# Axial attention: score matmuls for two groups at once, reciprocals spread by full-array matmuls, value loads issued by SyncE

## The chip, the cores and the metric

One Trainium2 chip, one core of it. The time is the device time of one execution in microseconds (us), as the median of several runs. The kernel is one launch; it computes four residual layers on a batch of four images with 256 channels of 64 x 64 pixels, all in float32 outside.

## The reference

Each layer is `x = x + f(groupnorm(x))`. The change concerns layer 0, an axial attention along the image's rows; the other three are 3x3 convolutions (one with ternary weights, one with binary activations, one with weights built from 4 x 4 scales). Cut to what matters:

```
q, k, v = bn1(einsum('nci,oc->noi', x, w_qkv))      # n = 256 rows of pixels, 16 groups,
                                                    # q and k 8 channels, v 16, i = 64 positions
qe = einsum('ngci,cij->ngij', q, q_emb)             # q_emb[c,i,j] = rel[c, i-j+63]
ke = einsum('ngci,cij->ngij', k, k_emb)
qk = einsum('ngki,ngkj->ngij', qe, ke)
sim = bn2(concat([qk, qe, ke], axis=1)).sum over the three
sim = softmax(sim, axis=3)                          # over j
attn   = einsum('ngij,ngcj->ngci', sim, v)
attn_e = einsum('ngij,cij->ngci', sim, v_emb)
out = bn3(concat([attn, attn_e])), the two halves added
```

The batch normalisations use the statistics of this batch, so each needs all of its input before it can be applied.

## The kernel before, in words

The program is written with a tile framework: the code issues instructions in a program order, a planner orders them per engine with that order as priority, and it puts in the semaphore waits. DMAs are issued from two queues, SP (SyncE, `nc.sync`) and ACT (ScalarE, `nc.scalar`); a DMA issued from ACT stands in line with ACT's own instructions. All DMAs of both queues share eight completion semaphores in turn, and each waits for the DMA before it on its own semaphore.

Scratch tensors in device memory (DRAM) carry data between the stages. A *pair* gp (0 to 7) is two of the sixteen groups, r = 0 and 1.

**Stage A** (L154 to L328, 0 to 317 us): group norm and the projection of q, k, v (L257). The projections of one image lie in `qs`, 128 partitions x 8 x 512, and are stored to `q_d` by sixteen DMAs from ACT (L295 to L299), one for each of two halves t (q and k channels) and eight l (the position i modulo 8). The values go to `vt_d`.

**Stage B** (L350 to L618, 317 to 1076 us): the products `qk`. `projections(j)` (L388) loads `qb` from `q_d` by two SP DMAs for four groups (L393), 32 DMAs in all, and DVE scales it (L399). `position_terms` multiplies with the relative embeddings `rm` into `pd` (PE, L434) and DVE transposes that into `t` (L441). `product` (L445 on) multiplies the transposed terms (PE, L453) into `pq`; ACT copies `pq` to the output tile `o` with a sum (L457) and squares it in place for a second sum (L462). `o` holds one pair of one image (128 partitions x 4096 numbers, 2 MB) and has two buffers (pool `op`), `pq` has two PSUM banks. There are 4 x 8 = 32 such tiles. A finished tile is stored to `qk_d` in four parts of 512 KB from ACT, one after each of the first four products of the next tile (`finish`, L522 to L527), and the last tile by one DMA of 2 MB (L559). The order of the loop (L535 to L556): position terms of half a tile, then two products of the half before, and so on. `term_sums` and the pieces of work called `jobs` (weights of a later layer) lie between.

**Stage C** (L621 to L893, 1076 to 1700 us): eight units, each one image and half of the pairs (four of them). A partition of the large tile `pt` is one group r of a pair and one position j, as 64 r + j; its columns are the pairs, rows n and positions i. In each unit:
- `scores(u, k)`, k = 0 to 7: `terms` (L676) loads `qc` by one SP DMA of 512 KB for two k and ACT applies the batch norm to it in eight activations (L687); SP loads `si`, 1 MB of `qk_d` (L699; three buffers, pool `cip`); PE adds the two embedding terms by sixteen matmuls of 32 rows x 64 columns of the array, 256 wide, for r = 0 and 1, two parities of i and four row groups of the array (L711, tile `e`); DVE adds `si` into `pt` (L723).
- `exponentials`: ACT, four activations for a k (L753). `sums`: PE adds up over the 64 j by matmuls with ones (L764, `den`).
- `reciprocals` (L771): DVE inverts `den`; PE spreads the result to the 16 channels of each group by 64 matmuls of 32 x 32 for each half h of a tile, in two PSUM tiles `pr` (L784); ACT copies it to `rb` (L789).
- `values` (PE L796) with the value matrices `vb`, `values_out` (DVE L805, then an ACT DMA to `at_d`), and `embedded` (PE L820, DVE L826) with the matrices `ve`.
- `load_values` (L663) loads the `vb` of the next unit by sixteen ACT DMAs of 128 KB (L667); they are called in fours between the `values_out` of this unit. `vb` is zeroed once by POOL (L637).

The order: scores of the next unit are interleaved with `embedded` of this one. `cnt` (L653) holds two constant matrices, `ones` for the sums and `pick` for the spreading. A second version of stage C with shifted exponentials (`general`) stands behind a branch that isn't taken here. The convolutions follow from 1700 us to the end.

Of the kernel before, what the change touches and what calls it, by code (L numbers as in the profile page):

```python
# [32 lines left out]
M_ID, M_GRP, M_GRPS, M_ALL, M_TKC, M_KTC, M_SHUF, M_ODD, M_N = 0, 1, 2, 3, 4, 6, 8, 9, 10  # L33

GROUPS = [0, 1, 2, 3, 8, 9, 10, 11, 4, 5, 6, 7, 12, 13, 14, 15]


@with_exitstack
def network(ctx: ExitStack, tc, x, wqkv, relm, relt, relw, relv, counts, masks, vecs, rowv, ab, w1, l2w1, l2w2, l3w, mats, out):
# [12 lines left out]
    q_d = [scratch(f"q_d{b}", [8, 2, 8, G, 512]) for b in range(B)]  # L52
# [84 lines left out]
    def kernel_rows(u, w, a, c):  # L137

        v = nc.vector
        v.tensor_scalar(u[:, 0], w[:, 0], 0.25, None, ALU.mult)  # L140
        v.tensor_copy(u[:, 5], w[:, 2])
        v.tensor_tensor(a, w[:, 0], w[:, 2], ALU.add)
        v.tensor_tensor(u[:, 1], a, w[:, 1], ALU.add)
        v.tensor_tensor(u[:, 2], a, w[:, 1], ALU.subtract)
        v.tensor_scalar(u[:, 1:3], u[:, 1:3], -1.0 / 6, None, ALU.mult)
        v.scalar_tensor_tensor(c, w[:, 2], 4.0, w[:, 0], ALU.mult, ALU.add)
        v.scalar_tensor_tensor(u[:, 3], w[:, 1], 2.0, c, ALU.mult, ALU.add)
        v.scalar_tensor_tensor(u[:, 4], w[:, 1], -2.0, c, ALU.mult, ALU.add)
        v.tensor_scalar(u[:, 3:5], u[:, 3:5], 1.0 / 24, None, ALU.mult)

# [5 lines left out]
    with ExitStack() as ph:  # L156
# [86 lines left out]
        for b in range(B):  # L243
# [51 lines left out]
            for t in range(2):  # L295
                for l in range(8):
                    nc.scalar.dma_start(
                        out=q_d[b][l, t].rearrange("c g f -> g c f"), in_=qs[t][:, l].rearrange("p a h -> p (a h)")
                    )  # L299
# [30 lines left out]
    def spread_scales(sp, psp, xs, order, tag="pst"):  # L330


        ps = psp.tile([P, 2, G], F32, name=fresh(tag), tag=tag)
        for t in range(2):
            r = small(sp, [P, 2, G])
            for i in range(2):
                nc.vector.tensor_scalar(r[:, i, :], msk, xs[t][:, i : i + 1], None, ALU.mult)
            nc.tensor.matmul(
                ps.rearrange("p i g -> p (i g)"), lhsT=mt[:, order + t, :], rhs=r.rearrange("p i g -> p (i g)"),
                start=(t == 0), stop=(t == 1),  # L340
            )
        s = small(keep, [P, 2, G])
        nc.vector.tensor_copy(s, ps)
        return s
# [8 lines left out]
    with ExitStack() as ph:  # L353
# [30 lines left out]
        sq = spread_scales(sp, psq, xs1, M_TKC, "pq")  # L384
# [3 lines left out]
        def projections(j):  # L388

            b, s = divmod(j, 4)  # L390
            q = bqp.tile([P, 4, 8, 64], F32, name=f"qb_{j}", tag="qb")
            for t in range(2):
                nc.sync.dma_start(  # L393
                    out=q[64 * t : 64 * t + 64].rearrange("p g a n -> p (g a n)"),
                    in_=q_d[b][:, t, :, 4 * s : 4 * s + 4].rearrange("l c g f -> l c (g f)"),
                )
            for g in range(4):
                c = 4 * s + g
                nc.vector.tensor_scalar(  # L399
                    q[:, g], q[:, g], sq[:, 0, c : c + 1], sq[:, 1, c : c + 1], ALU.mult, ALU.add  # L400
                )
            return q
# [115 lines left out]
        def finish(step, k):  # L518
            ts, o, b, gp, nb = step
            product(ts, o, 4 * nb + k, 8 * b + 4 * nb + k, gp, f"{b}_{gp}")  # L520

            if whole:  # L522
                wb, wgp, wo, part = whole[0]
                nc.scalar.dma_start(
                    out=qk_d[wb][wgp][:, bass.ts(part, 1024)],
                    in_=wo[:, 8 * part : 8 * part + 8].rearrange("p a n b -> p (a n b)"),
                )  # L527
                whole[0] = (wb, wgp, wo, part + 1)
                if part == 3:
                    whole.pop()  # L530
            if nb == 1 and k == 3:
                whole.append((b, gp, o, 0))
# [26 lines left out]
        nc.scalar.dma_start(out=qk_d[B - 1][GP - 1], in_=o.rearrange("p a n b -> p (a n b)"))  # L559
# [27 lines left out]

        s2q = small(keep, [P, GP])
        for r in range(2):
            rows = slice(64 * r, 64 * r + 64)  # L590
            nc.vector.tensor_copy(s2q[rows], s2[rows, 0:G].rearrange("p (a r) -> p a r", r=2)[:, :, r])

        def term_scales(coef):
# [9 lines left out]
            return spread_scales(sp, pss, xs, M_KTC)  # L603
# [31 lines left out]
    for m in range(4):  # L635
        for r in range(2):
            nc.gpsimd.memset(vb[m][64 * r : 64 * r + 64, :, :, 16 - 16 * r : 32 - 16 * r, :], 0.0)  # L637
# [6 lines left out]
    rw = cp_.tile([P, 2, 127], F32, name="rw")  # L644
# [4 lines left out]
    for r in range(2):  # L649
        src = bass.AP(tensor=relv.tensor, offset=relv.offset, ap=[[16, 64], [16, 64], [1, 16]])  # L650
        nc.sync.dma_start(out=ve[64 * r : 64 * r + 64, :, 16 * r : 16 * r + 16], in_=src)
    cnt = cp_.tile([P, 2, 16, 32], F32, name="cnt")
    nc.sync.dma_start(out=cnt, in_=counts)  # L653
    ones, pick = cnt[:, 0], cnt[:, 1]
    units = [(b, th) for b in range(B) for th in range(2)]

    def attention(general, good):
# [5 lines left out]
        def load_values(u, m):  # L663
            b, th = units[u]
            for r in range(2):
                for h in range(2):
                    nc.scalar.dma_start(  # L667
                        out=vb[m][64 * r : 64 * r + 64, h, :, 16 * r : 16 * r + 16, :]
                        .rearrange("p a c m -> p a (c m)"),
                        in_=vt_d[b][m, r, 64 * h : 64 * h + 64, 4 * th : 4 * th + 4]  # L670
                        .rearrange("p a c m -> p a (c m)"),
                    )
# [3 lines left out]
        def terms(u, m):  # L676

            b, th = units[u]
            q = qp.tile([P, 8, 2, 64], F32, name=f"qc_{b}_{th}_{m}_{general}", tag="qc")
            qf = q.rearrange("p g a n -> p g (a n)")  # L680
            nc.sync.dma_start(
                out=qf,
                in_=q_d[b].rearrange("l t c g f -> (l t c) g f")[:, 8 * th : 8 * th + 8, bass.ts(m, P)],
            )
            for g in range(8):
                k = 8 * th + g
                nc.scalar.activation(  # L687
                    qf[:, g], qf[:, g], AF.Identity, bias=scale_e[:, 1, k : k + 1], scale=scale_e[:, 0, k : k + 1]
# [3 lines left out]
        def scores(u, k):  # L692
# [13 lines left out]
            for par in range(2):  # L706
                for r in range(2):
                    for x_ in range(4):
                        rows = slice(32 * x_, 32 * x_ + 32)
                        i = 8 * k + 2 * x_ + par  # L710
                        nc.tensor.matmul(  # L711
                            es[x_ // 2][64 * r : 64 * r + 64, x_ % 2, :, :, par],
                            lhsT=rw[rows, par, 63 - i : 127 - i],
                            rhs=q[rows, :, k % 2, :].rearrange("p (a r) n -> p r a n", r=2)[:, r],
                            start=True, stop=True, tile_position=(32 * x_, 64 * r),
                        )
# [14 lines left out]
        def shifted(u, k):  # L731
            for i in range(4 * k, 4 * k + 4):
                for a in range(4):
# [4 lines left out]
                    nc.vector.tensor_reduce(m, ps.rearrange("p (r j) -> p r j", r=2), AX.X, ALU.max)  # L738
                    mb = wp.tile([P, 2, 64], F32, name=f"mb_{u}_{i}_{a}", tag="mb")
                    nc.vector.tensor_copy(mb, m.unsqueeze(2).to_broadcast([P, 2, 64]))  # L740
                    ps = pso.tile([P, P], F32, name=f"sm_{u}_{i}_{a}", tag="o")
                    nc.tensor.matmul(ps, lhsT=mb.rearrange("p r j -> p (r j)"), rhs=ident, start=True, stop=True)
# [27 lines left out]
        def reciprocals(u, h):  # L770
# [8 lines left out]
            for y in range(2):  # L779
                ps = pse.tile([P, 8, P], F32, name=f"pr_{u}_{h}_{y}_{general}", tag="e")  # L780
                for i in range(8):
                    for a in range(4):
                        rows = slice(32 * a, 32 * a + 32)
                        nc.tensor.matmul(  # L784
                            ps[rows, i, :], lhsT=pick[rows, 8 * y + i, :], rhs=rd[rows, :],
                            start=True, stop=True, tile_position=(32 * a, 32 * a),
                        )
# [674 lines left out]
def _matrices():  # L1462
# [8 lines left out]
    m[:, M_ODD] = p[None, :] == 2 * (p[:, None] % 64) + 1  # L1471
    for t in range(2):
        same = p[:, None] % 8 == p[None, :] % 8
        m[:, M_TKC + t] = same & (p[None, :] // 64 == t)
        m[:, M_KTC + t] = same & (p[None, :] // 8 % 2 == t)
# [3 lines left out]
def _counts():  # L1479

    ones = np.zeros((2, 64, 16, 16, 2), np.float32)
    pick = np.zeros((4, 16, 2, 16, 2, 16), np.float32)
    for r in range(2):
        for s in range(16):
            ones[r, :, s, s, r] = 1
            pick[:, s, r, s, r, :] = 1
    return np.stack([ones.reshape(P, 16, 32), pick.reshape(P, 16, 32)], axis=1)


def _embeddings(rel):  # L1490

    m = np.zeros((2, 8, 8, 120, 8), np.float32)
    w = np.zeros((8, 2, 8, 2, 127), np.float32)
    for k in range(8):
        m[:, k, :, :, k] = rel[:, :, k : k + 120][:, :, ::-1]
        w[k, :, :, k % 2, :] = rel[:, :, ::-1]
    at = np.arange(64)[None, :] - np.arange(64)[:, None] + 63
    t = rel[:, :, at].transpose(2, 3, 0, 1).reshape(64, 8, 8, 2, 8).transpose(0, 1, 3, 2, 4)
    return {"relm": m.reshape(P, 120, 8), "relt": t.reshape(64, 8, P), "relw": w.reshape(P, 2, 127)}
# [68 lines left out]
```

## Time and profile before

| | us |
|---|---|
| median of 3 runs | 3138.52 (3137.96 to 3145.68) |
| the profiled execution | 3136.36 |
| its span from first to last instruction | 3134.5 |
| stage A | 0 to 317 |
| stage B | 317 to 1076 |
| stage C | 1076 to 1700 |
| convolutions | 1700 to 3134 |

The page of the profile gives busy time by engine (PE is TensorE's matmul, PEld its weight load, DVE VectorE, ACT ScalarE, POOL GpSimd, SP SyncE), the DMA queues (q1 is SP's, q10 ACT's, q8 fetches PE's instructions), then groups of instructions, one row for each line, engine and operation: the tile written and those read, the shape, how many, their busy time and mean, and behind the bar the idle time of the engine just before them and what ended it. "issue" is a wait for nothing that the profile shows. Two rows as an example, those of the scores and of the spreading in stage C, here in an answer that is narrowed to 1100 to 1700 us:

```
L711 PE MATMUL e_False<-qc_False,rw 32*64 32x256 f32 x2048 | 115.4, 431 | 23.7 <-ACT qc_False L687 11.8 <-issue 6.2 <-DVE pt L723 3.0
L784 PE MATMUL pr_False<-rd_False,cnt 32*32 32x128 f32 x2048 | 65.9, 276 | 7.1 <-issue 5.6 <-DVE rd_False L773 1.1
```

"32*64" is the part of the array that the matmul uses. A float32 product counts as two instructions in these rows: stage C has 1024 such score matmuls in the code and 2048 in the trace. Several small matmuls run at once in different parts of the array, so that the busy time of a group isn't the sum of its means. "_False" in a name is the version without the shift.

The windows view gives, for any stretch, each engine's busy time, the granted clock of PE, the share of time in which the sixteen DMA engines were busy (1.0 is all sixteen) and the GB/s they moved.

### The profile page before, as it was taken

To read this page: it belongs to the slowest core of one execution; us is meant where nothing else is said; L and a number is where in the kernel's file an instruction comes from. 1 tells how busy PE (TensorE), PEld (TensorE's weight loads), DVE (VectorE), ACT (ScalarE), POOL (GpSimd) and SP (SyncE) were. 2 spreads that over 40 slices of the span, in tenths; PEclk is the share of its full clock that TensorE was granted. 3 is DMA by queue.
4 is the path that set the end of the run, shared out by engine and by line. 5 is a ranking of instruction groups with operands and counts; after the bars stand their busy time and mean duration, and the time that the engine had idled before them with its cause. 6 is when DMAs were issued, how large, how long until landed. Compare 5 with 4: busy or idle time off the path is not lost. (4 is left out here: it accounts for less than half of the span.)

```text
span 3134.5 us, 82495 instructions
## 1 busy us (share of the span) xinstructions
PE 2658.2 (85%) x36800; PEld 1594.8 (51%) x36800; DVE 2069.3 (66%) x3554; ACT 1118.0 (36%) x2201; POOL 44.1 (1%) x101
## 2 busy tenths in 40 slices
PE   6889887898899777777774699999996885999999
PEld 3445555666667655565563244444453452444443
DVE  5642599565556545655566889887587768778653
ACT  3334344444455455555540110101167931101010
POOL 0000000000000100000000000000000000000000
PEclk9999899898999989999997799999998997999999
DMA  5764435423323557776765454340434644333200
GB/s 210 224 215 119 120 140 192 145 105 109 136 97 138 144 188 241 253 249 224 243 204 204 143 159 139 113 151 27 154 125 155 231 171 156 134 127 116 92 41 40
DMA packets 245993, 484.04 MB, mean 154 GB/s; under 512 B 27200, under 2 KB 125632, under 8 KB 225792
## 3 DMA queue, kind: packets, MB, share of 16 engines
q1 hardware_dynamic: 139952, 327.68, 31.3%
q10 hardware_dynamic: 105680, 151.02, 13.9%
q8 instruction: 291, 4.77, 0.6%
q14 instruction: 70, 0.57, 0.1%
HBM read 282.28 MB, written 196.35 MB: 153 GB/s over the span
## 5 line engine op out<-in xcount | busy, mean ns | idle before, releaser
L959 PE MATMUL gc<-gtr,g_u 128*128 128x512 f32 x1152 | 502.4, 598 | 20.6 <-issue 13.0
L959 PE MATMUL dc<-dtr,d_u 128*128 128x512 f32 x1152 | 504.0, 598 | 17.1 <-DVE dtr L945 11.6
L441 DVE STREAM_TRANSPOSE t<-pd 128x1024 f32<-128x1024 f32 x256 | 303.8, 1225 | 100.4 <-PE pd L434 100.4
L959 PEld LDWEIGHTS gc<-gtr,g_u 128*128 128x128 f32 x1152 | 219.1, 191 | 296.1 <-issue 283.6
L959 PEld LDWEIGHTS dc<-dtr,d_u 128*128 128x128 f32 x1152 | 218.0, 191 | 289.0 <-issue 265.3
L434 PE MATMUL pd<-rm,qb 64*32 64x256 f32 x8192 | 299.0, 406 | 76.7 <-DVE t L441 75.8
L453 PEld LDWEIGHTS pq<-t,t 64*64 64x64 f32 x8192 | 263.6, 138 | 75.5 <-issue 45.1
L1191 PE MATMUL pc<-e_tr,e_k 128*64 128x512 bf16 x2304 | 266.4, 392 | 39.1 <-ACT pc_o L1199 20.5
L453 PE MATMUL pq<-t,t 64*64 64x64 f32 x8192 | 282.6, 222 | 17.6 <-issue 14.8
L457 ACT ACTIVATE o<-pq 128x512 f32<-128x512 f32 x256 | 151.9, 594 | 332.2 <-PE pq L453 332.1
L434 PEld LDWEIGHTS pd<-rm,qb 64*32 64x32 f32 x8192 | 160.5, 112 | 167.1 <-DVE t L441 95.5
L753 ACT ACTIVATE pt<-pt,sm 128x512 f32<-128x512 f32 x256 | 162.7, 709 | 194.1 <-DVE pt L723 116.5
L1191 PEld LDWEIGHTS <-e_k 128*64 128x64 bf16 x2304 | 156.1, 113 | 148.1 <-issue 51.5
L723 DVE TENSOR_TENSOR pt<-e_False,si_False 128x1024 f32<-128x1024 f32 x128 | 150.5, 1217 | 62.6 <-PE e_False L711 62.5
L257 PE MATMUL po<-xg,wt 128*128 128x512 f32 x256 | 129.7, 643 | 28.9 <-ACT qs L261 24.8
L462 ACT ACTIVATE pq<-pq 128x512 f32<-128x512 f32 x256 | 149.4, 584 | 6.1
L820 PE MATMUL pe_False<-pt,ve 128*32 128x64 f32 x4096 | 93.9, 235 | 57.2 <-issue 50.5
L977 ACT COPY gc_c<-gc 128x512 f32<-128x512 f32 x32 | 18.6, 580 | 344.2 <-PE gc L959 344.2
L764 PE MATMUL den_False<-pt,cnt 128*32 128x128 f32 x2048 | 110.7, 297 | 35.2 <-ACT pt L753 33.5
L977 ACT COPY dc_c<-dc 128x512 f32<-128x512 f32 x32 | 18.6, 583 | 329.3 <-PE dc L959 329.3
L711 PE MATMUL e_False<-qc_False,rw 32*64 32x256 f32 x2048 | 115.4, 431 | 23.7 <-ACT qc_False L687 11.8
L796 PE MATMUL pa_False<-pt,vb 128*32 128x64 f32 x4096 | 103.1, 242 | 33.4 <-issue 28.4
(376 smaller groups left out, 3456.9 us busy)
## 6 DMA issues: line engine op xcount, KB each, us to landing
si_False<-qk_d SPq DMA_DIRECT2D x64, 1024.0 KB
qk_d<-o ACTq DMA_DIRECT2D x124, 512.0 KB
x<-x_d SPq DMA_DIRECT2D x32, 1056.0 KB
a<-at_d SPq DMA_DIRECT2D x256, 128.0 KB
xa<-in_x SPq DMA_DIRECT2D x16, 1024.0 KB
vt_d<-vs ACTq DMA_DIRECT2D x32, 512.0 KB
q_d<-qs ACTq DMA_DIRECT2D x64, 256.0 KB
qb<-q_d SPq DMA_DIRECT2D x32, 512.0 KB
```

The lines of the kernel that those rows point to most:

```text
L257: nc.tensor.matmul(psf, lhsT=wt[:, t, bass.ts(o, P)], rhs=xg[:, t, :], start=(t == 0), stop=(t == 1))
L434: nc.tensor.matmul(pds[t][32 * c : 32 * c + 32, m].rearrange("p j k -> p (j k)"), lhsT=q[rows, 2 * (gp % 2) + g, a, 32 * nb : 32 * nb + 32 ...
L441: nc.vector.transpose(ts[t][:, :, 32 * jh : 32 * jh + 32].rearrange("p a j b -> p j a b"), pds[t].rearrange("p m j k -> p j m k"),)
L453: nc.tensor.matmul(ps[rows, m, :], lhsT=ts[1][rows, n // 2, :, n % 2], rhs=ts[0][rows, n // 2, :, n % 2], start=True, stop=True, tile_posi ...
L457: nc.scalar.activation(o[:, :, 8 * k : 8 * k + 8, :], ps.rearrange("p n (a b) -> p a n b", b=2), AF.Copy, accum_out=acc[:, 0, gp, col : co ...
L462: nc.scalar.activation(psf, psf, AF.Square, accum_out=acc[:, 1, gp, col : col + 1])
L711: nc.tensor.matmul(es[x_ // 2][64 * r : 64 * r + 64, x_ % 2, :, :, par], lhsT=rw[rows, par, 63 - i : 127 - i], rhs=q[rows, :, k % 2, :].re ...
L723: nc.vector.tensor_tensor(dst, e, src, ALU.add)
L753: nc.scalar.activation(s, s, AF.Exp, scale=s2q[:, gp : gp + 1])
L764: nc.tensor.matmul(dens[u, h][32 * a : 32 * a + 32], lhsT=ones[:, i, :], rhs=pt[:, 16 * h + i, a].rearrange("p n b -> p (n b)"), start=(i ...
L959: nc.tensor.matmul(ms[k], lhsT=u[:, t, dx, k, bass.ts(co, P)], rhs=vs[t][:, k, :, dx : dx + 64], start=(first and dx == 0), stop=(last and ...
L1191: nc.tensor.matmul(m[64 * g : 64 * g + 64], lhsT=parts[:, g, i, k, dx, :], rhs=vs[g][:, k, 8 * (q % 2) : 8 * (q % 2) + 8, dx : dx + 64], s ...
```

## The change

- A pair's groups are interleaved in stage C: a partition is 2 j + r in place of 64 r + j, in `pt`, `vb`, `ve`, `ones` and `s2q`. So that `si` arrives in this order, the store of `qk_d` writes row 2 j + r of DRAM from partition 64 r + j.
- The scores of both groups come from one matmul of 32 rows x 128 columns: eight for a k in place of sixteen. `rw` holds the embeddings for both r side by side.
- `qc` is loaded by two DMAs for two k (one for each parity of i) in place of one, and scaled by four activations of 256 columns in place of eight of 128. For that, `q_d` has a new order of dimensions, and the eight l are permuted (even ones first, `EIGHT`). The store of `q_d` and the loads of `qb` follow: each `qb` comes by eight DMAs of 128 KB in place of two of 512 KB.
- The reciprocals are spread by 16 matmuls of the whole array for each half tile, in place of 64 of 32 x 32. `cnt` grows from 512 KB to 1.25 MB.
- The `vb` loads are issued from SP in place of ACT, and write every second partition; the zeroing of `vb` is four memsets of a whole tile in place of eight of a part.
- Small things once in the kernel: the scales of pairs are spread by four small matmuls in place of two, `s2q` is made by two DVE operations on all partitions, and the matrices `mt` go from ten to twelve.

The core of the diff:

```diff
-    q_d = [scratch(f"q_d{b}", [8, 2, 8, G, 512]) for b in range(B)]
+    q_d = [scratch(f"q_d{b}", [GP, 8, 2, 2, 8, 512]) for b in range(B)]
...
-                        out=q_d[b][l, t].rearrange("c g f -> g c f"), in_=qs[t][:, l].rearrange("p a h -> p (a h)")
+                        out=q_d[b][:, l, t].rearrange("a r c f -> a (r c) f"),
+                        in_=qs[t][:, EIGHT[l]].rearrange("p a h -> p (a h)"),
...
-                nc.sync.dma_start(
-                    out=q[64 * t : 64 * t + 64].rearrange("p g a n -> p (g a n)"),
-                    in_=q_d[b][:, t, :, 4 * s : 4 * s + 4].rearrange("l c g f -> l c (g f)"),
-                )
+                for g in range(4):
+                    nc.sync.dma_start(
+                        out=q[64 * t : 64 * t + 64, g].rearrange("p a n -> p (a n)"),
+                        in_=q_d[b][2 * s + g // 2, :, t, g % 2],
+                    )
...
-                    out=qk_d[wb][wgp][:, bass.ts(part, 1024)],
+                    out=qk_d[wb][wgp].rearrange("(j r) f -> r j f", r=2)[:, :, bass.ts(part, 1024)],
                     in_=wo[:, 8 * part : 8 * part + 8].rearrange("p a n b -> p (a n b)"),
...
-        nc.scalar.dma_start(out=qk_d[B - 1][GP - 1], in_=o.rearrange("p a n b -> p (a n b)"))
+        nc.scalar.dma_start(
+            out=qk_d[B - 1][GP - 1].rearrange("(j r) f -> r j f", r=2), in_=o.rearrange("p a n b -> p (a n b)")
+        )
...
-        for r in range(2):
-            rows = slice(64 * r, 64 * r + 64)
-            nc.vector.tensor_copy(s2q[rows], s2[rows, 0:G].rearrange("p (a r) -> p a r", r=2)[:, :, r])
+        nc.vector.tensor_scalar(s2q, s2r[:, 0], even, None, ALU.mult)
+        nc.vector.scalar_tensor_tensor(s2q, s2r[:, 1], odd, s2q, ALU.mult, ALU.add)
...
-        for r in range(2):
-            nc.gpsimd.memset(vb[m][64 * r : 64 * r + 64, :, :, 16 - 16 * r : 32 - 16 * r, :], 0.0)
+        nc.gpsimd.memset(vb[m], 0.0)
...
-        nc.sync.dma_start(out=ve[64 * r : 64 * r + 64, :, 16 * r : 16 * r + 16], in_=src)
-    cnt = cp_.tile([P, 2, 16, 32], F32, name="cnt")
+        nc.sync.dma_start(out=ve[r:P:2, :, 16 * r : 16 * r + 16], in_=src)
+    cnt = cp_.tile([P, 16, 32 + P], F32, name="cnt")
     nc.sync.dma_start(out=cnt, in_=counts)
-    ones, pick = cnt[:, 0], cnt[:, 1]
+    ones, pick = cnt[:, :, 0:32], cnt[:, :, 32 : 32 + P]
...
-                    nc.scalar.dma_start(
-                        out=vb[m][64 * r : 64 * r + 64, h, :, 16 * r : 16 * r + 16, :]
+                    nc.sync.dma_start(
+                        out=vb[m][r:P:2, h, :, 16 * r : 16 * r + 16, :]
...
-            q = qp.tile([P, 8, 2, 64], F32, name=f"qc_{b}_{th}_{m}_{general}", tag="qc")
-            qf = q.rearrange("p g a n -> p g (a n)")
-            nc.sync.dma_start(
-                out=qf,
-                in_=q_d[b].rearrange("l t c g f -> (l t c) g f")[:, 8 * th : 8 * th + 8, bass.ts(m, P)],
-            )
-            for g in range(8):
-                k = 8 * th + g
+            q = qp.tile([P, 4, 2, 2, 64], F32, name=f"qc_{b}_{th}_{m}_{general}", tag="qc")
+            for par in range(2):
+                nc.sync.dma_start(
+                    out=q[:, :, par].rearrange("p a k n -> p a (k n)"),
+                    in_=q_d[b].rearrange("a (two k) t r c f -> two (k t r c) a f", two=2)[par][
+                        :, 4 * th : 4 * th + 4, bass.ts(m, P)
+                    ],
+                )
+            for a in range(4):
+                gp = 4 * th + a
+                qf = q[:, a].rearrange("p x k n -> p (x k n)")
                 nc.scalar.activation(
-                    qf[:, g], qf[:, g], AF.Identity, bias=scale_e[:, 1, k : k + 1], scale=scale_e[:, 0, k : k + 1]
+                    qf, qf, AF.Identity, bias=scale_e[:, 1, gp : gp + 1], scale=scale_e[:, 0, gp : gp + 1]
...
-                for r in range(2):
-                    for x_ in range(4):
-                        rows = slice(32 * x_, 32 * x_ + 32)
-                        i = 8 * k + 2 * x_ + par
-                        nc.tensor.matmul(
-                            es[x_ // 2][64 * r : 64 * r + 64, x_ % 2, :, :, par],
-                            lhsT=rw[rows, par, 63 - i : 127 - i],
-                            rhs=q[rows, :, k % 2, :].rearrange("p (a r) n -> p r a n", r=2)[:, r],
-                            start=True, stop=True, tile_position=(32 * x_, 64 * r),
-                        )
+                for x_ in range(4):
+                    rows = slice(32 * x_, 32 * x_ + 32)
+                    i = 8 * k + 2 * x_ + par
+                    nc.tensor.matmul(
+                        es[x_ // 2][:, x_ % 2, :, :, par], lhsT=rw[rows, 63 - i : 127 - i].rearrange("p j r -> p (j r)"),
+                        rhs=q[rows, :, par, k % 2, :], start=True, stop=True, tile_position=(32 * x_, 0),
...
-                    for a in range(4):
-                        rows = slice(32 * a, 32 * a + 32)
-                        nc.tensor.matmul(
-                            ps[rows, i, :], lhsT=pick[rows, 8 * y + i, :], rhs=rd[rows, :],
-                            start=True, stop=True, tile_position=(32 * a, 32 * a),
-                        )
+                    nc.tensor.matmul(ps[:, i, :], lhsT=pick[:, 8 * y + i, :], rhs=rd, start=True, stop=True)
```

## The prediction

> **What bounds the kernel now.** I read the page first (engine totals, DMA queues, issues), then the chain of waits, then busy time by stage, then the timeline where a stage waits. The chain that ended last names the convolutions (PE L959, L1191), which the edit leaves alone, so only stages A to C (0 to 1700 us) can move.
>
> ```profile
> PE 2658.2 (85%) x36800; PEld 1594.8 (51%) x36800; DVE 2069.3 (66%) x3554; ACT 1118.0 (36%) x2201; POOL 44.1 (1%) x101
> q10 hardware_dynamic: 105680, 151.02, 13.9%
> qk_d<-o ACTq DMA_DIRECT2D x124, 512.0 KB
> ```
>
> PE is busiest, and q10, ACT's queue, is light when averaged over sixteen engines. The stages, from the windows of busy time (columns: window, its length, PE, PEld, DVE, ACT, POOL, granted clock, DMA share, GB/s):
>
> ```profile
> 700.00:900.00 200.00, 164.50 (x4449) 124.44 (x4455) 112.55 (x183) 90.12 (x276) 0.00 (x0) 0.91 0.35 120
> 1311.00:1380.00 69.00, 55.23 (x1789) 42.47 (x1790) 41.14 (x51) 36.55 (x68) 3.95 (x8) 0.95 0.76 246
> 395.70:399.00 3.30, 3.03 (x80) 2.13 (x66) 3.30 (x8) 1.46 (x5) 0.00 (x0) 1.00 1.01 401
> 569.00:575.00 6.00, 4.68 (x136) 3.32 (x132) 0.58 (x1) 4.57 (x14) 0.00 (x0) 1.00 0.50 124
> ```
>
> Stage B (first row) is PE's: 164.5 of 200 us, DMA 0.35. A stage C unit (second; eight units of about 70 us) has PE busy 55 of 69, in alternation with DVE and ACT. The last two rows decide my forecast. While four `qk_d` stores run, all sixteen DMA engines are busy: 401 GB/s, 25 per engine. While `qb` is loaded alone, the share is 0.50: **eight of sixteen**. That load's source has l (8) as its slowest dimension. DVE feels it:
>
> ```profile
> 566.79 1.28 SPq L393 DMA_DIRECT2D qb<-q_d  x2
> 578.47 1.00 DVE L399 TENSOR_SCALAR qb<-qb,sm 128x512 f32<-128x512 f32 x2 [8.88 <-DMA qb<-q_d]
> DVE qb L399 <- DMA qb<-q_d: 76.0, 10, 9.6
> ```
>
> **What the Trainium skill says.** "DMA: Bandwidth & Descriptors", section "Why a DMA increments its semaphore by 16 and not by 1": a hardware-issued DMA uses the largest number of engines, at most 16, that divides the slowest non-1 dimension of both access patterns, and takes the lowest-numbered ones. The trace agrees: share 0.50 for an outer 8, and two `qb` loads post 16 completion writes, eight each, while four `qk_d` stores post 64. "Runtime: NRT & Kernel Launch", section "Instruction fetch mechanics": instructions come in 16 KiB blocks of 256, at a cost mostly hidden. Here the blocks are 16,384 B on q8, but not hidden: PE's "issue" gaps in stage C sum to some 88 us (L820 50.5, L796 28.4, L711 6.2, L784 5.6), each ending about 2.45 us after a fetch begins.
>
> **The change, part by part.**
>
> 1. *The `qk_d` store (L522-527, L559).* The DRAM side becomes [2, 64, 1024], r outermost; SBUF stays 128 partitions. By the rule two engines carry it, not sixteen. A 512 KB store is 128 packets of 4,096 B, each 159 ns in the trace's packet records: 8 x 0.159 = 1.3 us on sixteen engines, 64 x 0.159 = 10.2 us on two. An output tile `o` has four stores: 40.7 us. Compute needs 22.3 us a tile: part 0 of the stores is first issued at 394.75 and last at 1064.10, 30 intervals. `o` has two buffers, so ACT's L457 for tile n+1 waits until tile n-1 is stored; behind it on ACT stand L462, the other stores and, through the two `pq` banks, PE's products, then `t`, `pd` and DVE. So the stores set the period. To 40.7 I add the restart, in which the two engines stand idle (L457 to store issue 0.7 us, issue to first packet 0.87: 1.6), and engine 0's and 1's own part of the `qb` loads, 64 KB a tile, 32 packets at the 84 ns that `si`'s 2 KB packets take: 2.7. Period 45.0. Stage B is longer by 30 x (45.0 - 22.3) = **+681 us**. Lower bound: neither addend, 30 x 18.4 = +552. Upper: `qb` at the rate of its present packets (8,192 B in 549 ns: 4.4 us), a restart of 3 and packets 8% slower: 51.4, so +873. The last two tiles' stores, some 80 us, drain under the start of stage C, where five `si` loads find every packet on engines 0 and 1 paired with a store's: 32 x (84 + 159) ns = 7.8 us against the 3.6 us of a score step. At most 5 x 4.2 = 21, at least 0: **+15**.
>
> 2. *The `q_d` store (L295) and the `qb` loads (L391).* The store's outermost dimension goes from 16 to 8: 256 KB on eight engines, about 1.3 us instead of 0.7. 64 x 1.3 = 81 us under 317 us of stage A; ACT's L261 waits for it twice now (31.8 us in all). 0 to 20, I take **+5**. `qb`: 32 issues become 128 of 0.59 us, still eight engines, 2 KB packets: 4.7 us of issue per j where 1.2 stands. Landing 7 to 12 us against 11.7, worth -35 to +10 if compute set the period; under stores that do, 0. SP has nothing else due there but `u_d` and weights.
>
> 3. *Scores (L711).* 2048 matmuls become 1024, 64x32 tiles becoming 128x32. Half the calls, but four tiles now run at once where eight did: a `k` keeps its four rounds of 216 ns (256 columns each). "TensorE: Matmul & The Clock Gate", section "LDWEIGHTS (loading the stationary operand)", prices a load by its columns; the trace has 132 ns for 64 columns and 190 for 128, both below a 216 ns round. PE streaming: 0, at most +3 a unit.
>
> 4. *Reciprocals (L784).* 2048 become 512 full-array ones, 109 ns each for 128 columns either way (128 take 3.7 to 4.1 us). If the 190 ns load isn't hidden, 32 x 0.08 = 2.6 us, 16 times: +41; L414's 128-column loads are hidden today, but behind 216 ns. I take +0.3 us each, **+5**. `cnt` grows by 0.75 MB, once, before it is needed: 0.
>
> 5. *Instruction fetch.* 2560 fewer pairs of load and matmul in stage C: 20 of 112 blocks. In proportion 88 x 20/112 = -16; the stalls of L711 and L784, which no longer outrun the fetch, give -12. Together at most -28, and -45 if a freed fetch also arrives earlier for L820 and L796; **-22**.
>
> 6. *terms (L687).* 256 activations become 128 of twice the width. Eight take 3.2 us; I put four at 1.9 (estimate from 481 ns for 128 columns and 709 for 512). Of 32 x 1.3 = 42 us little is on the path, since ACT mostly waits for DVE's `pt` (116.5 us of L753's waits): **-8**, from 0 to -20. Two `qc` issues for one on SP: 32 x 0.4 us, prefetched: 0.
>
> 7. *Value loads (L667) from ACT to SP.* 128 issues of 0.63 us.
>
> ```profile
> L667 ACTq DMA_DIRECT2D vb<-vt_d x128: 580/627/1882, 1078.6 to 1608.4; - x128
> 1083.72 15.02 ACTq L667 DMA_DIRECT2D vb<-vt_d  x15
> 1098.79 9.34 ACT L687 ACTIVATE qc_False<-qc_False,sm 128x128 f32<-128x128 f32 x24 [14.83 <-DMA vb<-vt_d]
> ```
>
> At the start of stage C ACT issues fifteen of them for 15 us while the scales were ready at 1090.0: the first scaling starts 8.8 us earlier, and 24 scalings take 5.6 instead of 9.3: **-12**. In each later unit sixteen issues (10 us) leave ACT; L753 waits for them, and I count 1.15 us a unit: **-9**, from 0 to -25. On SP they pass in front of the next `si` loads (L699). Three `si` buffers are filled ahead, so 0; without that cover, up to 5 us a unit. The `vb` memsets on POOL (8.0 us in all) stay as long, hidden.
>
> Stage C: -22 - 8 - 12 - 9 + 5 = **-46** (from -90 to +20).
>
> **The sum.** The profiled execution took 3136.4 us (span 3134.5, 1.9 around it), 2.2 below the median of 3138.5. 3136.4 + 681 + 15 + 5 - 46 = 3791; with the 2 us to the median, **3793**.
>
> **The rivals.**
>
> *All engines still store `qk_d`* (the program's lowering turns the pattern round so that 64 or 128 is outermost). Then stage B stays PE's, and what shows is stage C: 3138.5 - 46 + 5 - 8 (earlier `qb`) = **3090**, faster. For it: the addresses allow it, and one reordering decides. Against it: `qb` has 64 partitions on its SBUF side and still runs on eight engines, so an outer dimension was not turned round there. It decides from the engine count: below 512 KB / 22.3 us x 4 = 94 GB/s, under four engines, the stores bind; with four or more they hide. 15%.
>
> *The two engines run at `qb`'s rate*, 15.5 GB/s each instead of 25, because the pace hangs on how few engines run or on the row strides: 262,144 B / 15.5 = 16.9 us a store, a period near 72, +1490, **4600**. For it: that is what eight engines did for `qb`. Against: that load reads 8 KB rows from DRAM; the store writes 4 KB rows as before. 3%.
>
> *SP becomes the late one in stage C*: 77 us of `vb` issues ahead of `si`, with stores at full width; -46 turns into about -5, **3138**. Against: three `si` loads and the `qc` are issued ahead of the value phase. 2%.
>
> **How the numbers follow.** Two engines, as summed: 80%, itself 3650 (item 1's lower bound, the rest as taken, without the +15: 3138.5 + 552 + 5 - 46) to 3985 (its upper: 3138.5 + 873 + 15 + 5 - 46). Full width 15%, `qb`'s rate 3%, SP 2%. The range of 3650 to 3990 is the first case's; the 20% left out are the others, all too far off to reach. Faster by over 0.3% (9 us, about what a measurement of this kernel can tell from no change): 0.15; within: 0.02; slower: 0.83.
>
> **What would show it.** After: stage B ends near 1760 instead of 1079; in it the DMA share is about 2/16 = 0.13 to 0.2; ACT's L457 waits for DMA `qk_d<-o`, about 30 times some 20 us; q10's share of packet time stays near 14%, since the packets are the same. Stage C units take 64 to 66 us, `e_False` and `pr_False` have x1024 and x512, and `vb` stands under SPq. It is wrong if DMA's share is near 1 while a store runs, or if L457 still waits for `pq`.

## The result and the profile after

The changed kernel takes 3784.16 us (median of 4 runs, 3781.32 to 3789.05); the kernel before, beside it, 3138.24. The ratio is **1.206** (95% interval 1.203 to 1.209): slower, as forecast, at 9 us from the predicted 3793. The profiled execution spans 3779.5 us against 3134.5: +645.0.

From the page, the engines, ACT's queue and the stores again, and now also ACT's copy into `o`:

```profile
PE 2713.6 (72%) x34248; PEld 1662.6 (44%) x34248; DVE 2073.2 (55%) x3555; ACT 1081.3 (29%) x2073; POOL 43.6 (1%) x97
q10 hardware_dynamic: 68602, 134.23, 9.5%
L465 ACT ACTIVATE o<-pq 128x512 f32<-128x512 f32 x256 | 151.6, 593 | 977.3 <-issue 512.7
qk_d<-o ACTq DMA_DIRECT2D x124, 512.0 KB
```

PE has nearly the work it had (2714 us to 2658) in a span a fifth longer: something else holds it. The row of L465 (L457 before) says where: ACT stood idle 977 us ahead of it, 513 of them for nothing that the profile names.

The windows, with the columns as in the prediction: all of stage B in the kernel before (first to last product), then, of the changed kernel, a stretch within stage B, all of stage B, from there to DVE's first addition into `pt`, and stage C from there to the first convolution matmul.

```profile
372.30:1078.30 706.00, 614.13 (x16454) 464.25 (x16452) 483.87 (x820) 343.05 (x1045) 3.32 (x3) 0.94 0.36 128
1120.00:1140.00 20.00, 4.29 (x67) 4.15 (x67) 2.38 (x2) 2.46 (x8) 0.00 (x0) 0.57 0.13 53
396.10:1726.80 1330.70, 671.63 (x16454) 511.10 (x16452) 487.94 (x822) 341.09 (x1046) 5.29 (x3) 0.74 0.18 68
1726.80:1784.90 58.10, 6.92 (x44) 5.50 (x40) 6.18 (x37) 8.90 (x18) 3.54 (x2) 0.53 0.16 54
1784.90:2377.70 592.80, 448.02 (x11776) 367.32 (x11776) 362.50 (x503) 259.83 (x415) 32.27 (x70) 0.87 0.74 245
```

In the second line, DMA's share is 0.13, two of sixteen engines, moving 53 GB/s; while four stores ran before, it was 1.01 and 401. Stage B as a whole has a share of 0.18 and takes 1331 us, where it took 706. The granted clock is lower too, 0.74 for 0.94, but PE's busy time in stage B grew by only 58 us (614 to 672): the clock can be only a small part of the 625.

The timeline of ACT inside stage B, and of DVE at the start of stage C, shows who stands behind the stores:

```profile
1135.10 8.29 ACTq L532 DMA_DIRECT2D qk_d<-o  x1
1157.07 10.42 ACTq L532 DMA_DIRECT2D qk_d<-o  x1
```

```profile
1784.95 2.36 DVE L734 TENSOR_TENSOR pt<-e_False,si_False 128x1024 f32<-128x1024 f32 x2 [44.42 <-DMA qk_d<-o]
```

The *issue* of a store now lasts 8 to 10 us on ACT, about as long as a store of 10.2 us; before, the median was 0.4. That is the "issue" in L465's row. And stage C's first addition waits 44 us for the last store, which ends at 1784.3.

Stage times of every kernel of this study, each from its own trace (us; "to B" is the time of the first product, "gap" from the last product to the first addition into `pt`, "C" from there to the first matmul of the convolutions):

| kernel | to B | B | gap | C | rest | span |
|---|---|---|---|---|---|---|
| before | 372.3 | 706.1 | 25.7 | 628.6 | 1401.9 | 3134.5 |
| after | 396.1 | 1330.8 | 58.1 | 592.8 | 1401.8 | 3779.5 |
| e1_split | 394.4 | 683.7 | 17.3 | 591.6 | 1398.9 | 3085.8 |
| e2_two | 368.7 | 1330.8 | 73.8 | 632.4 | 1401.7 | 3807.4 |
| e3_four | 369.4 | 757.6 | 51.2 | 626.7 | 1402.1 | 3207.1 |
| e10_eight | 372.5 | 727.2 | 38.9 | 642.9 | 1400.6 | 3182.0 |
| e4_last | 398.5 | 1329.0 | 24.5 | 599.8 | 1399.9 | 3751.7 |
| e5_vb_act | 394.6 | 684.8 | 24.4 | 578.6 | 1400.1 | 3082.5 |
| e6_recip | 392.6 | 693.5 | 17.1 | 617.9 | 1400.5 | 3121.5 |
| e7_scores | 396.3 | 682.0 | 16.8 | 603.2 | 1402.0 | 3100.4 |
| e8_qd_sp | 374.4 | 682.5 | 17.3 | 598.9 | 1401.7 | 3074.7 |
| e9_mix | 374.7 | 690.8 | 17.3 | 583.4 | 1403.7 | 3069.9 |
| e11_mix_recip | 375.1 | 692.3 | 17.0 | 600.9 | 1403.2 | 3088.5 |
| e12_mix_scores | 373.9 | 686.2 | 16.8 | 605.5 | 1403.2 | 3085.6 |

### The profile page after: what moved, and what is told of

Same layout as the page of the kernel before. It is cut to its first block, busy times and chain, and to the rows that moved or that the text cites. A ratio compares the mean times of both kernels' runs of the same rounds, so it can differ in the third digit from the quotient of the medians.

```text
span 3779.5 us, 77460 instructions
## 1 busy us (share of the span) xinstructions
PE 2713.6 (72%) x34248; PEld 1662.6 (44%) x34248; DVE 2073.2 (55%) x3555; ACT 1081.3 (29%) x2073; POOL 43.6 (1%) x97
## 5 line engine op out<-in xcount | busy, mean ns | idle before, releaser
L461 PE MATMUL pq<-t,t 64*64 64x64 f32 x8192 | 324.7, 240 | 376.9 <-ACT pq L470 374.8
L965 PE MATMUL dc<-dtr,d_u 128*128 128x512 f32 x1152 | 503.9, 598 | 17.1 <-DVE dtr L951 11.6
L461 PEld LDWEIGHTS pq<-t,t 64*64 64x64 f32 x8192 | 303.0, 155 | 440.4 <-ACT pq L470 416.5
L465 ACT ACTIVATE o<-pq 128x512 f32<-128x512 f32 x256 | 151.6, 593 | 977.3 <-issue 512.7
L1197 PE MATMUL pc<-e_tr,e_k 128*64 128x512 bf16 x2304 | 266.3, 392 | 38.9 <-ACT pc_o L1205 20.2
L427 DVE SCALAR_TENSOR_TENSOR pr<-ptq,qb 128x256 f32<-128x256 f32 x128 | 46.6, 420 | 394.9 <-PE ptq L422 394.9
L407 DVE TENSOR_SCALAR qb<-qb,sm 128x512 f32<-128x512 f32 x64 | 33.5, 542 | 291.3 <-DMA qb<-q_d 281.2
L724 PE MATMUL e_False<-qc_False,rw 32*128 32x256 f32 x1024 | 127.8, 478 | 68.1 <-DVE pt L734 57.0
L260 PE MATMUL po<-xg,wt 128*128 128x512 f32 x256 | 130.0, 645 | 45.4 <-ACT qs L264 41.3
L275 PE MATMUL pv<-wt,xg 128*128 128x256 f32 x512 | 124.7, 387 | 0.0
```

The costliest lines, as they stand in the source:

```text
L260: nc.tensor.matmul(psf, lhsT=wt[:, t, bass.ts(o, P)], rhs=xg[:, t, :], start=(t == 0), stop=(t == 1))
L275: nc.tensor.matmul(pv[:, j, :], lhsT=xg[:, t, pix], rhs=wt[:, t, C : 2 * C], start=(t == 0), stop=(t == 1),)
L461: nc.tensor.matmul(ps[rows, m, :], lhsT=ts[1][rows, n // 2, :, n % 2], rhs=ts[0][rows, n // 2, :, n % 2], start=True, stop=True, tile_posi ...
L465: nc.scalar.activation(o[:, :, 8 * k : 8 * k + 8, :], ps.rearrange("p n (a b) -> p a n b", b=2), AF.Copy, accum_out=acc[:, 0, gp, col : co ...
L724: nc.tensor.matmul(es[x_ // 2][:, x_ % 2, :, :, par], lhsT=rw[rows, 63 - i : 127 - i].rearrange("p j r -> p (j r)"), rhs=q[rows, :, par, k ...
L965: nc.tensor.matmul(ms[k], lhsT=u[:, t, dx, k, bass.ts(co, P)], rhs=vs[t][:, k, :, dx : dx + 64], start=(first and dx == 0), stop=(last and ...
```

## The experiments

The theory: the store of `qk_d` runs on two engines and sets stage B's pace. The rival: the other changes in stages A and B (eight `qb` loads for two, the order of `q_d`) carry a good part.

**The store back on sixteen engines (e1_split).** The one edit, here and for the last store likewise:

```diff
-                nc.scalar.dma_start(
-                    out=qk_d[wb][wgp].rearrange("(j r) f -> r j f", r=2)[:, :, bass.ts(part, 1024)],
-                    in_=wo[:, 8 * part : 8 * part + 8].rearrange("p a n b -> p (a n b)"),
-                )
+                for r in range(2):
+                    nc.scalar.dma_start(
+                        out=qk_d[wb][wgp].rearrange("(j r) f -> r j f", r=2)[r][:, bass.ts(part, 1024)],
+                        in_=wo[64 * r : 64 * r + 64, 8 * part : 8 * part + 8].rearrange("p a n b -> p (a n b)"),
+                    )
```

> The changed kernel with each store of qk_d cut into two, one for each r, of 64 partitions and 64 rows: the slowest dimension of both sides is 64, so sixteen engines carry it. Nothing else is changed. Store theory: stage B falls back from 1348 us to 723 (-625) and the 32 us at the start of stage C go, so 3784 - 657 = 3127, down to 3100 if the smaller qb loads end DVE's waits; stage A's 24 us and stage C's -36 us stay. Rival (the eight qb loads per step or the new q_d order carry a good part of stage B's time): above 3300.

Measured: 3089.38 us, ratio to the kernel before 0.988 (0.985 to 0.991). The same bytes go to the same rows, and stage B falls from 1331 to 684 us, the gap from 58 to 17. The rival is out. It is also faster than both kernels; B is 22 us shorter than before, and with it DVE's waits for `qb` go from 76.0 us to 43.5. That these waits are the reason was not tried alone:

```profile
L407 DVE TENSOR_SCALAR qb<-qb,sm 128x512 f32<-128x512 f32 x64 | 33.1, 538 | 43.9 <-DMA qb<-q_d 43.5
```

**The store alone in the kernel before (e2_two).** With the order of instructions on every engine as before, and the last store changed likewise. Stage C still reads `qk_d` as it did, so it adds scores of other rows; only the time of this kernel counts:

```diff
-                    out=qk_d[wb][wgp][:, bass.ts(part, 1024)],
+                    out=qk_d[wb][wgp].rearrange("(j r) f -> r j f", r=2)[:, :, bass.ts(part, 1024)],
```

> The kernel before with only the store of qk_d written with r outermost, [2, 64, 1024]; every engine's order of instructions stays as before. The rows of qk_d then lie in another order than stage C reads, so the attention adds scores of other rows; the work is the same. Store theory: stage B +625 and the wait at the start of stage C +32, so 3138 + 657 = 3795 (3750 to 3840). Rival as for the first run: at most 3600.

Measured: 3810.10, ratio 1.218 (1.214 to 1.222), +682 us. B is 1330.8 us, to a tenth that of the changed kernel: this store alone makes stage B's loss. The waits, of ACT and behind it:

```profile
ACT o L457 <- issue: 812.0, 49, 29.7
PEld pq L453 <- ACT pq L462: 617.2, 127, 25.0
DVE pr L419 <- PE ptq L414: 586.1, 30, 23.6
```

ACT sits in the issues, PE waits for ACT to free `pq`, DVE for PE. The gap is 16 us longer than in the changed kernel. Here the `vb` loads are still issued from ACT, and fifteen of these issues, right behind the last narrow store, last 59 us where they lasted 15 before. These loads are wide (sixteen engines) in both kernels. ACT's first scaling of `qc` stands behind them:

```profile
1708.66 59.39 ACTq L669 DMA_DIRECT2D vb<-vt_d  x15
1768.09 9.34 ACT L689 ACTIVATE qc_False<-qc_False,sm 128x128 f32<-128x128 f32 x24 [59.20 <-DMA vb<-vt_d]
```

So the issue of a wide load grows too, when it follows a narrow store. In the changed kernel, SP has these loads.

**Four and eight engines (e3_four, e10_eight).** Both stores with `r=4` and with `r=8`, otherwise the kernel before; stage C again adds scores of other rows.

> As the second, but the outermost dimension is 4 (rows in yet another order, same work). Store theory: four engines, 32 packets of 159 ns = 5.1 us a store, 20.4 us a tile, just below the 22.3 us that compute needs, so stage B is nearly as before, and the last 2 MB take 32 x 0.61 = 20 us instead of 5: 3140 to 3190. Rival (what costs is any store on fewer engines, by its long issue on ACT, not the rate): time in proportion, 3138 + 657/3 = 3350 or more.

> As the second run (the kernel before, order of instructions unchanged), with an outermost dimension of 8 for the store of qk_d; the rows of qk_d again lie in another order than is read. Eight engines: 2.5 us a store, 10.2 us a tile against 22.3. Store theory: stage B as before, the last store 10 instead of 5 us: 3138 to 3145. If the 86 us of the run with four engines came from something else than the rate (the order of the rows, or where they lie in DRAM), part of it stays: above 3160.

Measured: 3213.79 with four, ratio 1.028 (1.025 to 1.032); 3177.69 with eight, 1.013 (1.010 to 1.015). Both lie above what I expected from the rate alone. The number of engines is as meant: in the packet records a store of 512 KB ends with 16 completion writes before, and with 2, 4 and 8 in e2, e3 and e10. The loss falls from 682 to 86 us between two and four engines, and 3214 is far from the 3350 of a loss in proportion, so the rate is the main thing: four engines need 20.4 us a tile where compute needs 22.3. But the loss isn't gone, and e10, above 3160, says by its own expectation that part of it isn't the rate. With four, the period is 24.1 us. What fills the 3.7 us above 20.4 isn't shown: by the packet records the store queue is without any packet for only 0.9 us a tile. The waits of ACT, first with four and then with eight:

```profile
ACT o L457 <- DMA qk_d<-o: 84.5, 14, 15.8
```

```profile
ACT o L457 <- issue: 58.9, 17, 3.7
```

With eight engines ACT's L457 no longer waits for the store, but stands up to 3.7 us behind the issue of one, for instance where two parts come close together: the two issues take 3.31 us of ACT at 607.83 in its trace.

```profile
607.83 3.31 ACTq L524 DMA_DIRECT2D qk_d<-o  x2
611.34 0.60 ACT L457 ACTIVATE o<-pq 128x512 f32<-128x512 f32 x1 [3.45 <-issue]
```

B is 21 us longer, the gap 13. The longer gap, here and with four engines (25 more), is mostly the `vb` issues on ACT again, which took 15.02 us before; first four, then eight:

```profile
1135.64 37.31 ACTq L669 DMA_DIRECT2D vb<-vt_d  x15
```

```profile
1105.99 27.25 ACTq L669 DMA_DIRECT2D vb<-vt_d  x15
```

The 14 us more in C with eight, where no such store runs, I can't explain. The three parts add to 49 where the medians differ by 40; this profiled execution was 6 us above its median. The other order of rows in DRAM is an unlikely reason: e2 and e3 have such an order too, and C at 632 and 627 (before 629), and the median store packet takes 159 ns in all four kernels.

**What the start of stage C waits for (e4_last).** The changed kernel with the edit of e1 for the last store, 2 MB, only.

> The changed kernel with only the very last store of qk_d, 2 MB, cut into two for sixteen engines; the order of instructions is the same. In the changed kernel DVE's first addition into pt waits 44 us until this store has ended (1784.3). If the wait is for the memory of o, which pt takes over, it ends when the store before it has drained, some 39 us earlier: 3784 - 39 = 3745. If it is for si, whose packets share the two engines, it hardly moves: 3775 to 3784.

Measured: 3750.58, ratio 1.198 (1.195 to 1.202) against 1.206. The gap falls from 58.1 to 24.5, as the first theory has it. DVE's wait of 44.42 us becomes 5.86:

```profile
1751.95 2.35 DVE L736 TENSOR_TENSOR pt<-e_False,si_False 128x1024 f32<-128x1024 f32 x2 [5.86 <-DMA qk_d<-o]
```

The first write of `pt` waits for a store that only reads `o`. It isn't a wait for late `si`: in the changed kernel the first three of these loads were issued between 567.4 and 580.4. It fits `pt` lying where `o` lay, but this isn't shown: the addition waits for all eight completion semaphores, of which the last store's came last, and neither tile was moved.

**Stage A (e8_qd_sp).** e1 with `nc.sync` in place of `nc.scalar` in the store of `q_d`.

> The first run's kernel with the stores of q_d issued from SP instead of ACT. Stage A ends some 18 us later than in the kernel before, and the first product 22. If this is ACT standing in the issue of twelve stores on eight engines at the end of stage A (17.4 us), it goes: 3089 - 18 = 3071. If it is the engines' rate that holds the q tile's buffer, it stays: 3085 to 3095.

Measured: 3076.05, ratio 0.979 (0.976 to 0.981) against 0.988. The first product comes at 374.4 us instead of 394.4. ACT's last twelve issues took 17.38 us in the changed kernel (11.36 before); now SP has them all, and longer, with nobody behind it:

```profile
344.02 24.73 SPq L300 DMA_DIRECT2D q_d<-qs  x16
```

So what e8 wins back is time that ACT stood in the issues of stores that run on eight engines. That the whole loss is of this kind isn't shown. The last projection matmul (`po`, so stage A lasts beyond the 317 us of the table of stages) ends at 336.7 before, at 354.2 in the changed kernel and at 343.9 in e8, so 7 us of the loss stay there, where ACT's copies into `qs` wait 41.3 us in all for these stores to end (31.8 before); e8 makes up for them since SP also takes the 11.36 us of issues that ACT had before.

**The value loads (e5_vb_act, e9_mix).** e1 with the `vb` loads on ACT again; then e8 with those of the first unit on SP and the others on ACT.

> The first run's kernel (stores of qk_d cut in two) with the vb loads issued from ACT again. By the prediction the move was worth 12 us at the start of stage C and 9 in its units: 3089 + 21 = 3110, units at 67 us and the gap before the first addition longer by some 8 to 12 us. Rival (ACT has slack everywhere but at the start): 3089 + 9 = 3098. Second rival (on SP the loads cost as much as on ACT): 3089.

> The first run's kernel with the stores of q_d from SP (as in the eighth run), and the vb loads from SP only for the first unit, from ACT for the others. If both findings add up (q_d from SP 17 us less to the first product; vb on ACT 2.6 us less a unit, vb on SP 7 us less at the start): ratio to the kernel before 0.975 to 0.976, some 3063. If the shorter units of the fifth run were chance: as the eighth run, 0.979.

Measured: e5 3092.08, ratio 0.985 (0.983 to 0.987), to be set beside e1's 0.988 (0.985 to 0.991); e9 3071.65, ratio 0.980 (0.978 to 0.982), beside e8's 0.979. Moving them makes no difference that shows in the time. In the profiles the first unit on SP shortens the gap (17 for 24 us), and C is shorter by 13 and 15 with the others on ACT; the medians don't bear out a gain from the mixture, so I don't count it. e8 and e9 are the fastest kernels here, and can't be told apart.

**Fewer instructions (e6_recip, e7_scores, e11_mix_recip, e12_mix_scores).** In e6 and e11 the reciprocals are spread by small matmuls again; in e7 and e12 each score matmul is cut in two. e6 and e7 start from e1, e11 and e12 from e9.

```diff
-                    nc.tensor.matmul(ps[:, i, :], lhsT=pick[:, 8 * y + i, :], rhs=rd, start=True, stop=True)
+                    for a in range(4):
+                        rows = slice(32 * a, 32 * a + 32)
+                        nc.tensor.matmul(
+                            ps[rows, i, :], lhsT=pick[rows, 8 * y + i, rows], rhs=rd[rows, :],
+                            start=True, stop=True, tile_position=(32 * a, 32 * a),
+                        )
...
-                        es[x_ // 2][:, x_ % 2, :, :, par], lhsT=rw[rows, 63 - i : 127 - i].rearrange("p j r -> p (j r)"),
-                        rhs=q[rows, :, par, k % 2, :], start=True, stop=True, tile_position=(32 * x_, 0),
+                            es[x_ // 2][:, x_ % 2, 2 * d : 2 * d + 2, :, par],
+                            lhsT=rw[rows, 63 - i : 127 - i].rearrange("p j r -> p (j r)"),
+                            rhs=q[rows, 2 * d : 2 * d + 2, par, k % 2, :],
```

> The first run's kernel with the reciprocals spread by 64 matmuls of 32 x 32 for each half tile again: 1536 more pairs of load and matmul in the trace, 12 more blocks of instructions. If the gain of stage C comes from fewer instruction blocks: 12/20 of the 29 us by which PE's issue gaps fell, 3089 + 15 = 3104. If a 190 ns load behind a 109 ns matmul costs what I put at 5 us, and no block matters: 3084.

> The first run's kernel with each score matmul cut into two of 128 columns of the moving side: 1024 more pairs in the trace, 8 more blocks, the same columns streamed, twice the loads of 128 columns. Fetch theory: 8/20 of 29 us, 3089 + 12 = 3101. Load theory (a load of 185 ns isn't hidden behind a round of 109): a k takes 8 rounds of up to 190 instead of 4 of 216, up to +0.7 us for 64 k, 3089 + 45 = 3134, less where DVE sets the pace. Neither: 3089.

> The ninth run's kernel with the reciprocals by 64 small matmuls again, to be read against the ninth, on the same chip. Fetch theory: +15 us (ratio +0.005), PE's issue gaps in stage C up by some 15; the sixth run's profile had stage C longer by 26 and its median only by a few. If the full-array form pays nothing: within 5 us of the ninth.

> The ninth run's kernel with each score matmul cut into two of 128 moving columns, to be read against the ninth. Fetch theory: +12 us. If the number of score matmuls doesn't matter: within 5 us of the ninth.

Measured: e6 3111.74, ratio 0.989 (0.986 to 0.992), and e7 3105.52, ratio 0.990 (0.987 to 0.993): beside e1's 0.988, which ran with another set of runs, inconclusive. On the same chip as e9 the difference is clear: e11 3091.96, ratio 0.986 (0.984 to 0.989), +20 us; e12 3088.89, ratio 0.985 (0.983 to 0.987), +17 us. The rows of PE in stage C, e9's and then e11's, show where:

```profile
L805 PE MATMUL pa_False<-pt,vb 128*32 128x64 f32 x4096 | 101.2, 242 | 25.0 <-issue 19.3 <-DVE o_False L814 5.2
L829 PE MATMUL pe_False<-pt,ve 128*32 128x64 f32 x4096 | 89.6, 240 | 33.8 <-issue 23.9 <-PEq L900 5.1 <-DVE o_False L814 4.6
L796 PE MATMUL pr_False<-rd_False,cnt 128*128 128x128 f32 x512 | 64.1, 285 | 4.1 <-issue 1.8 <-DVE pt L737 1.2 <-DVE rd_False L787 1.1
```

```profile
L727 PE MATMUL e_False<-qc_False,rw 32*128 32x256 f32 x1024 | 119.9, 443 | 22.2 <-issue 10.4 <-ACT rb L803 5.3 <-DVE pt L737 2.9
L810 PE MATMUL pa_False<-pt,vb 128*32 128x64 f32 x4096 | 106.5, 248 | 29.7 <-issue 24.3 <-DVE o_False L819 3.7 <-DVE st L824 1.6
L834 PE MATMUL pe_False<-pt,ve 128*32 128x64 f32 x4096 | 86.2, 235 | 34.9 <-issue 28.8 <-PEq L905 4.7 <-DVE o_False L840 1.0
L798 PE MATMUL pr_False<-rd_False,cnt 32*32 32x128 f32 x2048 | 64.3, 276 | 10.0 <-issue 7.8 <-DVE rd_False L787 1.1 <-DVE pt L737 1.1
```

PE's busy time for the spreading is the same, 64.1 and 64.3 us, for 512 and 2048 instructions: no work was saved. Its gaps marked "issue" grow, for `pe` too, whose code is the same: over `e`, `den`, `pa`, `pe` and `pr` from 54 to 76 us, and to 67 in e12. This is the wait for instruction blocks. Between 1070 and 1690 us q8 fetched 95 blocks in e9, 107 in e11 and 103 in e12, and 38 of e9's 41 gaps, 55 of e11's 61 and 43 of e12's 52 end 2.2 to 2.8 us after a fetch begins. The amounts (22 and 13) come near the lost 20 and 17. In e12 the doubled loads of 128 columns could have a part as well.

## Why the prediction was right, step by step

| term | predicted | measured |
|---|---|---|
| stage A, store of `q_d` | +5 | +24 |
| stage B, store of `qk_d` | +681 | +625 |
| start of C: last stores, less the earlier start | +15 - 12 | +32 |
| the units of stage C | -34 | -36 |
| sum | +655 | +645 |

That the sum is 10 us off is luck: stage B was put 56 us too high, stage A and the start of stage C 19 and 29 too low. The main term and its mechanism were not luck.

- **The two engines** (item 1) were right, and by the mechanism given: share 0.13, 159 ns for a 4,096 B packet as before, ACT held, PE and DVE behind it. The size was off by 56 us in the addends. The period is 42.3 us, not 45.0. Stores alone make 40.7; the restart of 1.6 is all that the rest allows. The 2.7 us for `qb`'s packets cost nothing: DVE waited 281 us for `qb` in the changed kernel and 84 in e2, and B is the same. In the packet records, from 1115.1 to 1154.0, each of the two engines carried 236 store packets (37.5 us) and, by the eight-engine split, 43 of `qb`'s (3.6 us), 41.1 us of packets in 38.9. Packets of the two queues ran side by side. Against this, ACT held in the issues makes the last tile 25 us longer (39.6 us from its first store issue to the last product, 14.2 before), where I had it unchanged.
- **The end of the stores** was mis-sized, and its mechanism failed: I had them drain under stage C at a cost through `si`. e1 has a gap of 17.3, 8 below that of before (predicted 12); the changed kernel's is 41 above e1's, where I had put 15. e4 shows the wait to be for the last store itself. I had not asked what the first write of `pt` waits for.
- **Stage A** failed: +24 lies outside my 0 to 20. I priced the engines' time (81 us under 317) but not ACT standing in each issue. e8 takes it away, in part with issues that ACT had before as well.
- **Stage C's units** came out in sum (mean unit 66.3 us after, 72.0 before, from one first addition to the next), not by parts. The rise of e11 (20) and of e12 (17) together has the size of the whole, though each was measured alone, beside e9; I had -22 for the fetch, +5 for the reciprocals. The fetch was mis-sized: PE's "issue" gaps in stage C fell by 37 us, from 92 to 55. My reading of them was a little off as well: the four parts add to 90.7, not 88, and 59 of the 65 gaps, not each, end 2.2 to 2.8 us after a fetch begins. The value loads, for which I had -9 in the units, brought nothing (e5, e9). The scaling of `qc` (the first 12 in 6.0 us after, the first 24 in 9.3 before) was not tried alone.
- **qb**: 0 under the stores, as said; with the store mended, -22 in B.
- **Signs I had named**: stage B ended at 1727 (1760), DVE's and PE's waits as said. ACT's wait showed as "issue" and only in part as a wait for `qk_d`. q10's share fell to 9.5% where I had "near 14": the 32,768 packets of `vb` had left it.
- **The rivals**: that all engines still store is what e1 makes, 3089, and I had put 3090 for it. This too is closer than the parts: stage A took 22 us more for my 5, B 22 less for my 8, and its ratio is 0.988 where 3090 makes 0.985. Its limit, "four or more hide", was wrong: four cost 86 us and eight 40, since narrow stores also lengthen the issues on ACT and, with four engines, still make it wait for `o`.

## What to carry to other kernels

Before a layout is changed for an engine's sake, look at the slowest dimension (the outermost that isn't 1) of every DMA that the layout touches, on both sides: here a rearrangement in a store's pattern took fourteen of sixteen DMA engines away, and two DMAs of 64 rows gave them back. A DMA in the queue of a compute engine costs that engine its issue, and the issue grows when transfers are narrow, that of a wide transfer behind a narrow one too. Also ask what the first write of the next stage waits for when a store is late. Fewer instructions with the same busy time can still pay where the instruction fetch shows as "issue" gaps.

## What the runs showed of the hardware that I had not expected

- The issue of a narrow store holds its engine: median 0.40 us with sixteen engines, 8.3 us with two (at most 19.4), and 2.9 at most with eight. Fifteen wide `vb` loads behind the last store took 15 us of issue before, and 27, 37 and 59 with the stores on eight, four and two engines.
- Packets of two queues went through at 159 ns and 84 ns, as they do alone, on two engines that by the eight-engine split had 41.1 us of them in 38.9.
- Half the engines were not enough for the stores, though DMA's share looks low: with eight it was 0.38 between 700 and 900 us, 0.35 before, and the kernel lost 1.3%. If `qb` runs on the same eight, they are busy for about 0.76 of the time (an estimate, twice 0.38).
- The `ve` load of 256 KB from SP, with stores on two engines beside it, held SP for 62 us (4.89 for two before).
